# Strassen's form for the output product of an attention kernel: seven products for two batches

## The chip, the cores and the metric

The kernel runs on one core of one Trainium2 chip. Its time is the device time of one execution in microseconds (us). The engines are named as the profile names them: PE (TensorE, matrix products), PEld (its weight loads), DVE (VectorE), ACT (ScalarE), POOL (GpSimd) and SP (SyncE, whose queue issues nearly all DMAs). All data is fp32.

## What is computed

64 batches of 128 tokens with 512 features pass through a multi-query attention with one null key, and are added to their input. There are 16 heads of 64, with keys and values shared by all heads.

```python
xn = layernorm(x, g_in)                       # x: 64 x 128 x 512
q = (xn @ Wq).reshape(b, n, 16, 64).transpose(0, 2, 1, 3) * 64 ** -0.5
k, v = split(xn @ Wkv)                        # one key head, one value head
k = concat([null_kv[0], k]); v = concat([null_kv[1], v])
sim = einsum('bhid,bjd->bhij', q, k) + concat([null_bias, attn_bias])
sim = where(causal or masked, -max, sim)
out = einsum('bhij,bjd->bhid', softmax(sim), v)
y = out.transpose(0, 2, 1, 3).reshape(b, n, 1024) @ Wo     # 1024 x 512
return x + layernorm(y, g_out)
```

The change concerns the second last line, the output product, and the layer norm after it.

## The kernel before

The order of all instructions is written out by hand: `step(n)` issues one step of a software pipeline, and each engine runs its own instructions strictly in the order in which `step` names them. One step holds work of several batches: the end of batch n-1 (output product, norm, residual, store), the values of batch n, the softmax of batch n+1, the scores of batch n+2, and the keys, values, token norms and loads of later batches. Query products are made for groups of four batches (GB = 4); `part` is the step's place in its group, and `qg` the group whose queries are being made.

The query product is already in Strassen's form with seven products (`product(g, f, k, ...)`, k from 1 to 7): operands are sums of weights (`wS`) and of tokens (`xS`, made by `token_sum` on POOL), the results are put together through PSUM accumulation, copies by ACT (`keep`, names p1, u2, u3) and additions by DVE (`q_out`). Below, q1 to q7 are these.

The names that matter around the change:

- `scores(b, hf)`: one half of the score rows on PE into a PSUM tile of pool `ps_s`, then DVE adds it to the bias (L495) and takes the row maxima (L496). `KEYS` says which half: 128 keys (`UK`, L474) or 64 keys (`LK`, L485). Before, half 0 is the one of 128 keys. `ps_s` has two buffers of two banks each.
- `bias_add(b)` (POOL, L445) writes bias plus mask into the score tile `S[b]`, and `null_copy(b)` (POOL, L454) the null key's columns, ahead of the scores.
- `exps(b, hf)` (ACT, L505): eight rows, each an exponential with a sum. `rinv` (DVE, L522) inverts the sums, `scale` (POOL, L526) multiplies the half by them.
- `blocks_T(b)` (DVE, L541) transposes `S[b]` in blocks of 32 into `sb`, and `blocks_move(b)` issues 14 DMAs on SP (L561) that put the blocks into `aTb`, of which there is one.
- `values(b)`: PE products of `aTb` (L610), ACT copies them to `oT[b]` (L618).
- `out_mm(b)` (PE, L630): eight 128 x 128 by 128 x 512 products of `oT[b]` and `wo` into one PSUM bank `py`. Each fp32 product appears in the trace as two instructions.
- `out_stats(b)`: DVE statistics of `py` (L637 to L641), the reciprocal root on POOL (L642), and one fused DVE pass that subtracts the mean and multiplies by the gain `gob` (L644). `residual(b)`: ACT multiplies by the reciprocal root (L658), POOL adds the input tile `res` (L659). `store(b)` issues the DMA.
- `norm_stats`, `norm_apply` (ACT, L249): the norm of the input tokens. `tokens_T`, `tokens_out`, `tokens_in`: their transposition through DRAM. `mask_neg` (DVE, L438): the mask of a group.

PSUM has eight banks: four for `ps_s`, two for `ps_q` (tags a and c), two for `ps_w` (tag w: the query product 2, `py`, the values and the key/value block in turn).

Of the kernel before, what the change touches and what calls it, by code (L numbers as in the profile page):

```python
# [8 lines left out]
FP = mybir.dt.float32  # L9
# [8 lines left out]
def kernel(  # L18
# [49 lines left out]

    nc = tc.nc
    B, N, DIM = x.shape
    H = attn_bias.shape[0]
    DH = w_kv.shape[1] // 2
    P = 128
# [19 lines left out]

    ctx.enter_context(tc.manual_schedule())
    const = ctx.enter_context(tc.tile_pool(name="const", bufs=1))
    ps_s = ctx.enter_context(tc.tile_pool(name="ps_s", bufs=2, space=PSUM))
    ps_q = ctx.enter_context(tc.tile_pool(name="ps_q", bufs=1, space=PSUM))
    ps_w = ctx.enter_context(tc.tile_pool(name="ps_w", bufs=2, space=PSUM))  # L100
    xp = ctx.enter_context(tc.tile_pool(name="xp", bufs=XB))
    rp = ctx.enter_context(tc.tile_pool(name="rp", bufs=2))
# [17 lines left out]
    gp = ctx.enter_context(tc.tile_pool(name="gp", bufs=2))  # L120

    def loads_late(n):
        if 0 <= n:
            load_res(n)
        for m in (n + 13, n + 14):
            if m < B and (m > 2 * GB + 2) == (m == n + 14):
                load_x(m)
# [212 lines left out]
    HK, HT, HF = KC // 2, TOK // 2, H * DH // 2  # L340
    lo_k, hi_k = slice(0, HK), slice(HK, KC)
    lo_t, hi_t = slice(0, HT), slice(HT, TOK)
    wS = const.tile([P, 4, HK, HF], FP, name="wS")
    a11, a12 = wq[:, lo_k, 0:HF], wq[:, hi_k, 0:HF]
    a21, a22 = wq[:, lo_k, HF:], wq[:, hi_k, HF:]
    s1, s2, s3, s4 = (wS[:, i] for i in range(4))
    xS, prod, kept = {}, {}, {}

    def q_tile(g):
# [20 lines left out]
        )  # L370

    def weight_sums():
        nc.vector.tensor_tensor(s3, a11, a21, ALU.subtract)
        nc.vector.tensor_tensor(s1, a21, a22, ALU.add)
        nc.vector.tensor_tensor(s2, s1, a11, ALU.subtract)
        nc.vector.tensor_tensor(s4, a12, s2, ALU.subtract)

    def token_sum(g, k):

# [41 lines left out]
    def q_out(g, c, toks, tag, name=None):  # L421
        lo = toks.start // N
        o = q_part(g, c, lo, lo + 2)
        p = prod[tag].rearrange("p (t h i) -> p t h i", t=2, h=2)
        if name is None:
            nc.scalar.copy(o, p)  # L426
        else:
            k = kept[name].rearrange("p (t h i) -> p t h i", t=2, h=2)
            nc.vector.tensor_tensor(o, p, k, ALU.add)  # L429


# [25 lines left out]
        )  # L457


    KEYS = UK, LK  # L460
    WITH_NULL = slice(1 + NL, ROW), slice(0, 1 + NL)

    def scores(b, hf):
        g, t = divmod(b, GB)
        nk = N if hf == 0 else NL
        ps = ps_s.tile([P, 2, NF, N], FP, tag="s", name=f"ps_{b}_{hf}")
        pv = ps.rearrange("p r f j -> p r (f j)")[:, :, 0 : NF * nk].rearrange(
            "p r (f j) -> p r f j", f=NF
        )
        for f in range(NF):  # L470
            if hf == 0:
                for r in range(2):
                    rows = slice(r * DH, (r + 1) * DH)
                    nc.tensor.matmul(  # L474
                        pv[:, r, f, :],
                        qT[g][rows, f, t, 1].rearrange("p u i -> p (u i)"),
                        kT[b][rows, :],
                        start=True,
                        stop=True,
                    )  # L480
            else:
                for r in range(2):
                    rows = slice(r * DH, (r + 1) * DH)
                    for u in range(2):
                        nc.tensor.matmul(  # L485
                            pv[u * DH : (u + 1) * DH, r, f, :],
                            qT[g][rows, f, t, 0, u],
                            kT[b][rows, 0:NL],
                            start=True,
                            stop=True,  # L490
                        )
        if hf == 0:
            nmax[b] = small.tile([P, 2, R8], FP, tag="nmax", name=f"nmax_{b}")
        sv = S[b][:, :, KEYS[hf]].rearrange("p (r f) j -> p r f j", r=2)
        nc.vector.tensor_tensor(sv, pv, sv, ALU.add)  # L495
        nc.vector.tensor_reduce(  # L496
            nmax[b][:, hf], S[b][:, :, WITH_NULL[hf]], AX.X, ALU.max, negate=True
        )

    def exps(b, hf):  # L500
        if hf == 0:
            rsum[b] = small.tile([P, 2, R8], FP, tag="rsum", name=f"rsum_{b}")
        for k in range(R8):
            row = S[b][:, k, WITH_NULL[hf]]
            nc.scalar.activation(  # L505
                row,
                row,
                AF.Exp,
                bias=nmax[b][:, hf, k : k + 1],
                accum_out=rsum[b][:, hf, k : k + 1],  # L510
            )
# [115 lines left out]
    def out_mm(b):  # L627
# [4 lines left out]
            )  # L632
        ys[b] = py

    def out_stats(b):
        st = small.tile([P, 6], FP, tag="st", name=f"sto_{b}")
        nc.vector.bn_stats(st, ys[b])  # L637
# [2 lines left out]
        rstd = small.tile([P, 1], FP, tag="rstdo", name=f"rstdo_{b}")  # L640
        nc.vector.tensor_scalar(rstd, mv[:, 1:2], EPS, None, ALU.add)  # L641
        nc.gpsimd.tensor_tensor(rstd, rstd, nhalf, ALU.pow)  # L642
        y = hp.tile([P, DIM], FP, tag="y", name=f"y_{b}")
        nc.vector.scalar_tensor_tensor(  # L644
            y, ys.pop(b), mv[:, 0:1], gob, ALU.subtract, ALU.mult
        )
# [56 lines left out]
    def step(n):  # L703
# [6 lines left out]
        q, f = ok(qg, NG), part  # L710
        last_g, last_f = divmod(n + 5, GB)
        fast, last = q and qg > 0, 0 < last_g < NG


        fill = n <= 0
        if part == 0 and ok(qg + 1, NG) and n + 6 >= 0:
            load_mask(qg + 1)
        if ok(n + 2) and n >= 0:
            bias_add(n + 2)
        for m in mns:  # L720
            norm_stats(m)
        if fast and f == 0:
            token_sum(qg, 1)
            if fill:
                for k in range(2, 5):
                    token_sum(qg, k)
        if n == -4:
            bias_add(0)
            bias_add(1)
        if ok(n + 2):  # L730
            null_copy(n + 2)
        if 2 * GB <= mb < B:
            tokens_T(mb)
            if (mb + 1) % GB == 0:
                tokens_out(mb // GB)
        if (n + 7) % GB == 0 and 2 <= (n + 7) // GB < NG:
            tokens_in((n + 7) // GB)
        if ok(n + 1) and not fill:
            exps_half(n + 1, 0)
            exps_half(n + 1, 1)  # L740
        if ok(n - 1):
            out_mm(n - 1)
            out_stats(n - 1)
        if fast and f == 0 and not fill:
            for k in range(2, 5):
                token_sum(qg, k)
        if last:
            product(last_g, last_f, 4, ps_q, "a", start=False)
            q_out(last_g, HC + last_f, lo_t, "a")
            product(last_g, last_f, 3, ps_q, "c", start=False)  # L750
            q_out(last_g, last_f, hi_t, "c", "u2")
        if ok(n + 1) and fill:
            exps_half(n + 1, 0)
        for m in mns:
            norm_apply(m)
        if part == 3 and ok(n + 3):
            nulls_move((n + 3) // GB, slice(0, GB - 1))
        if part == 0 and ok(n + 2):
            nulls_move((n + 2) // GB, slice(GB - 1, GB))
        if fast:  # L760
            if f == 0:
                q_tile(qg)
            product(qg, f, 2, ps_w, "w")
            product(qg, f, 1, ps_q, "a")
            keep("a", "p1")
            q_out(qg, f, lo_t, "w", "p1")
            product(qg, f, 5, ps_q, "c")
        elif q:
            q_plain(qg, 2 * f)
        if ok(n + 1) and fill:  # L770
            exps(n + 1, 1)
        if ok(n - 1) and q:
            residual(n - 1)
        if ok(n + 2):
            scores(n + 2, 0)
            if not q and n + 1 < B - 2:
                blocks_T(n + 1)
            if ok(n + 1) and fill:
                rinv(n + 1, 1)
                scale(n + 1, 1)  # L780
            scores(n + 2, 1)
        if n == B - 2:
            attn_T_pe(n)
        if ok(n):
            values(n)
        if ok(n - 1) and not q:
            residual(n - 1)
        if n + 1 in sbs:
            blocks_move(n + 1)
        if fast:  # L790
            product(qg, f, 6, ps_q, "a", start=False)
            keep("a", "u2")
        elif q:
            q_plain(qg, 2 * f + 1)
        if n + 10 < 2 * GB:
            norm_T(n + 10)
        if ok(mkv) and mkv >= GB - 1:
# [1 line left out]
            pk = ps_w.tile([P, KVN + N], FP, tag="w", name=f"pk_{mkv}")  # L799
            k_T(mk, pk[:, KVN:])  # L800
            kv_mm(mkv, pk[:, 0:KVN])
        if ok(n - 1):
            store(n - 1)
        loads_late(n)
        if ok(n + 1) and q and not fill:
            blocks_T(n + 1)
            blocks_move(n + 1)
        if ok(mkv) and mkv >= GB - 1:
            kT_out(mk, pk[:, KVN:])
            kv_out(mkv, pk[:, 0:KVN])  # L810
        if fast:
            product(qg, f, 7, ps_q, "a", start=False)
            keep("a", "u3")
        if ok(mk) and not ok(mkv):
            kT_out(mk, k_T(mk))
        if fast:
            q_out(qg, HC + f, hi_t, "c", "u3")
        if ok(n + 1) and fill:
            blocks_T(n + 1)
            blocks_move(n + 1)  # L820
        if n == -4:
            for m in range(GB - 1):
                kv_out(m, kv_mm(m))
                if m:
                    kT_out(m - 1, k_T(m - 1))
        if part == 3 and 0 < qg < NG:
            mask_neg(qg)

    def keep_busy(k):
# [95 lines left out]
```

## Time and profile before

| | us |
|---|---|
| median of three runs | 1198.63 |
| the three runs | 1196.96 to 1199.11 |
| the profiled execution | 1194.94 |
| its span in the profile | 1193.1 |
| PE busy in the span | 1151.9 (97%) |
| DVE, ACT, POOL busy | 716.2, 652.1, 654.4 |

The mean granted clock of PE was 0.991 of full speed. In a line of the page's groups or of the groups by form stand the source line, the engine, the operation, the tiles written and read, the shapes and the count; then total busy time and the mean in ns of one instruction; then the engine's idle time just before them with what ended it. A line of the timeline has start, length (both in us), engine, line, operation, tiles, shape and count of merged instructions. A line of the table by windows has the window, its length, the busy time of PE, PEld, DVE, ACT and POOL with counts, the clock, the DMA share and GB/s.

### The profile page before, as it was taken

The numbers are of one execution on the slowest core, as the hardware profiler recorded it, in microseconds if no ns is written. First come the engines' busy times: TensorE is split into PE (matmuls) and PEld (weight loads), VectorE is DVE, ScalarE is ACT, GpSimd is POOL, SyncE is SP. The second block draws the span as 40 slices with busy tenths as digits, with TensorE's granted clock in tenths as the row PEclk, the third lists the DMA queues.
The fourth block names the chain that finished last, engine by engine and source line by source line (L and its number), as shares of the span: only waits on it lengthen the run. The fifth ranks groups of instructions, "written<-read, shape, count | busy, mean of one in ns | idle before, by whom it ended". The sixth has DMA issues, their size and how long they took to land.

```text
span 1193.1 us, 22640 instructions
## 1 busy us (share of the span) xinstructions
PE 1151.9 (97%) x7588; PEld 747.9 (63%) x7588; DVE 716.2 (60%) x1449; ACT 652.1 (55%) x2625; POOL 654.4 (55%) x524
## 2 busy tenths in 40 slices
PE   6888999999999999999999999999999999999887
PEld 4465666666666666666666666666666666666433
DVE  6565566566666656656665665666566565545552
ACT  2254555565565556556555655655665565555551
POOL 5453755556475555647555465746546574654641
PEclk9998999999999999999999999999999999999999
DMA  6314334343533434343343434334353433422221
GB/s 185 111 39 127 96 124 122 119 122 90 143 95 122 121 112 130 90 136 103 122 115 116 131 91 133 105 123 111 111 140 90 130 99 106 102 74 71 70 81 45
DMA packets 107844, 129.79 MB, mean 109 GB/s; under 512 B 29264, under 2 KB 72528, under 8 KB 105936
## 3 DMA queue, kind: packets, MB, share of 16 engines
q1 hardware_dynamic: 106912, 127.29, 37.2%
q8 instruction: 61, 1.00, 0.4%
q10 hardware_dynamic: 816, 1.05, 0.2%
q14 instruction: 55, 0.45, 0.1%
HBM read 54.86 MB, written 31.46 MB: 72 GB/s over the span
## 4 chain that ended last, share of the span: by engine, by line
PE 86%; SPq 4%; DVE 2%; DMA 1%; issue 1%; ACT 0%; POOL 0%; DVEq 0%; ACTq 0%
PE py L630 35%; PE pa L408 17%; PE pc L408 8%; PE po L610 8%; PE ps L474 5%; PE pk L298 5%; PE pw L408 4%; SPq L561 4%; PE ps L485 3%; DMA aTb<-sb 1%; DVE sb L541 1%; PE pk L332 1%; DMA res<-in_x_dram 0%; DVE s L495 0%; PE paL L582 0%
## 5 line engine op out<-in xcount | busy, mean ns | idle before, releaser
L630 PE MATMUL py<-wo,oT 128*128 128x512 f32 x1024 | 453.6, 596 | 1.9 <-ACT oT L618 1.9
L445 POOL TENSOR_TENSOR s<-biasp,mneg 128x1536 f32<-128x1536 f32 x64 | 220.8, 3451 | 292.6 <-DVE sb L541 193.6
L505 ACT ACTIVATE s<-s,nmax 128x129 f32<-128x129 f32 (+1 forms) x1024 | 368.8, 365 | 0.0
L630 PEld LDWEIGHTS py<-wo,oT 128*128 128x128 f32 x1024 | 195.3, 191 | 223.9 <-issue 217.0
L526 POOL TENSOR_TENSOR s<-s,rinv 128x1024 f32<-128x1024 f32 (+1 forms) x128 | 188.4, 1479 | 15.5 <-DVE rinv L522 11.3
L505 ACT ACTIVATION_READ_ACCUMULATOR s<-s,nmax 128x1 f32 x1024 | 194.1, 190 | 0.0
L618 ACT ACTIVATE oT<-po,nv 128x512 f32<-128x512 f32 x128 | 81.3, 685 | 185.3 <-PE po L610 185.1
L495 DVE TENSOR_TENSOR s<-ps,s 128x1024 f32<-128x1024 f32 (+1 forms) x128 | 121.7, 951 | 68.9 <-PE ps L474 66.0
L659 POOL TENSOR_TENSOR y<-y,res 128x512 f32<-128x512 f32 x63 | 80.3, 1274 | 151.0 <-ACT y L658 151.0
L522 DVE RECIPROCAL rinv<-rsum 128x8 f32<-128x8 f32 x128 | 25.9, 203 | 209.7 <-ACT s L505 208.2
L408 PE MATMUL pa<-xS,wS 128*128 128x256 f32 x480 | 130.6, 395 | 0.7 <-ACT ku L419 0.7
L496 DVE TENSOR_REDUCE nmax<-s 128x8 f32<-128x1032 f32 (+1 forms) x128 | 123.1, 962 | 4.4
L610 PE MATMUL po<-aTb,vs 128*64 128x256 f32 (+1 forms) x768 | 109.8, 393 | 1.8 <-DVE aTb L589 1.7
L541 DVE STREAM_TRANSPOSE sb<-s 128x1536 f32<-128x1536 f32 x62 | 109.7, 1769 | 0.1
L419 ACT COPY ku<-pa 128x256 f32<-128x256 f32 x120 | 44.7, 373 | 116.1 <-PE pa L408 114.5
L408 PEld LDWEIGHTS pa<-xS,wS 128*128 128x128 f32 x480 | 83.0, 191 | 30.3 <-issue 20.0
L249 ACT ACTIVATE x<-x,nmr,rstd 128x512 f32<-128x512 f32 x60 | 48.7, 813 | 86.3 <-DVE nmr L248 85.9
L429 DVE TENSOR_TENSOR qT<-pw,kp 128x256 f32<-128x256 f32 x60 | 25.5, 425 | 98.5 <-ACT kp L419 98.5
L474 PEld LDWEIGHTS ps<-kT,qT 64*128 64x128 f32 x1024 | 62.5, 188 | 22.5 <-issue 21.8
L474 PE MATMUL ps<-kT,qT 64*128 64x128 f32 x1024 | 74.9, 286 | 0.0
L426 ACT COPY qT<-pa 128x256 f32<-128x256 f32 x60 | 22.4, 372 | 92.1 <-PE pa L408 92.1
L637 DVE BATCH_NORM_STATS2 sto<-py 128x6 f32<-128x512 f32 x64 | 44.8, 699 | 44.6 <-PE py L630 44.5
(90 smaller groups left out, 1547.4 us busy)
## 6 DMA issues: line engine op xcount, KB each, us to landing
aTb<-sb SPq DMA_DIRECT2D x372, 64.0 KB
x<-in_x_dram SPq DMA_DIRECT2D x64, 256.0 KB
res<-in_x_dram SPq DMA_DIRECT2D x64, 256.0 KB
out_dram<-y SPq DMA_DIRECT2D x64, 256.0 KB
aTb<-sb SPq DMA_DIRECT2D x496, 32.0 KB
xd<-xb SPq DMA_DIRECT2D x14, 1024.0 KB
xT<-xd SPq DMA_DIRECT2D x56, 256.0 KB
wo<-in_L_cond_Wo_dram SPq DMA_DIRECT2D x1, 2048.0 KB
```

Source lines behind the costliest of these rows:

```text
L408: nc.tensor.matmul(prod[tag], w[:, kc, f * P : (f + 1) * P], t[:, :, kc, :], start=(start and kc == 0), stop=(kc == HK - 1), skip_group_ch ...
L445: nc.gpsimd.tensor_tensor(S[b][:, :, 1 : ROW - 1], biasp, mneg[g][:, t].unsqueeze(1).broadcast_to([P, R8, NL + N]), ALU.add,)
L474: nc.tensor.matmul(pv[:, r, f, :], qT[g][rows, f, t, 1].rearrange("p u i -> p (u i)"), kT[b][rows, :], start=True, stop=True,)
L495: nc.vector.tensor_tensor(sv, pv, sv, ALU.add)
L496: nc.vector.tensor_reduce(nmax[b][:, hf], S[b][:, :, WITH_NULL[hf]], AX.X, ALU.max, negate=True)
L505: nc.scalar.activation(row, row, AF.Exp, bias=nmax[b][:, hf, k : k + 1], accum_out=rsum[b][:, hf, k : k + 1],)
L526: nc.gpsimd.tensor_tensor(sv, sv, rinvs.pop((b, hf)).unsqueeze(2).broadcast_to([P, R8, sv.shape[2]]), ALU.mult,)
L541: nc.vector.transpose(sb.rearrange("p j e q -> p e j q"), S[b][:, :, 1 : ROW - 1].rearrange("p e (j k) -> p e j k", k=Q),)
L610: nc.tensor.matmul(po[u][r * DH : (r + 1) * DH, half], vals, aTb[rows, slots, r * NF : (r + 1) * NF], start=True, stop=True,)
L618: nc.scalar.activation(oT[b][:, u * NF : (u + 1) * NF, :].rearrange("p f (s q) -> p s f q", q=Q), po[u].rearrange("p h i f q -> p (h i) f q"),
L630: nc.tensor.matmul(py, oT[b][:, c, :], wo[:, c, :], start=(c == 0), stop=(c == NC - 1))
L659: nc.gpsimd.tensor_tensor(y, y, res.pop(b), ALU.add)
```

## The change

Batches 1 to 60 are taken in pairs (p, p+1) with p odd. Their output products become one product of a 256 x 1024 matrix with a 1024 x 512 one, cut into two by two blocks: the rows by batch, the 1024 features in two halves of four chunks, the 512 outputs in two halves of 256. Strassen's form (Winograd's variant) needs seven block products of four 128 x 128 by 128 x 256 pieces each, where the plain form has eight. Batches 0, 61, 62 and 63 keep the plain form (`plain`).

The work of a pair is spread over three steps: products 1 and 2 in step p+1 (`first`), then in step p+2 (`second`) the sums of the stationary operands on POOL (`out_sums`, four passes over 128 x 512, in place in `oT`) and products 5, 6, 7 and 3, and in step p+3 (`third`) product 4, the norms and the residuals of both batches. So odd steps hold four of the products, even steps three.

What else moves:

- The results are put together in tags X and Y of a new PSUM pool `ps_y` (two banks), in ACT copies (yp1, yp5, one half of an output tile), one DVE copy (yu2) and three DVE additions (`out_part`). `ps_s` shrinks to one buffer for that.
- Of a paired batch the norm is no longer one fused DVE pass from PSUM and an ACT scale: ACT applies mean and scale (`pair_norm`), and POOL multiplies by `gob` and adds `res` (`pair_residual`).
- The 64-key half of the scores comes first now (`KEYS` is turned round), with the values between the two halves, and the exponentials are interleaved with the products.
- In odd steps `bias_add` and `null_copy` come behind the out_sums and the first `scale`, and `blocks_T` comes ahead of the scores' DVE work. In odd steps the query product 2 comes first.
- Token sums 1 and 2 of a group move to the end of the step before; 3 and 4 stay in the group's first step, ahead of the residuals on POOL.
- `load_res` of a paired batch comes a step later. The weight sum s3 is made in place on POOL; four sums of output weights (`wT`) are made on POOL in steps 0 to 3.

The diff, cut to its core:

```diff
-    ps_s = ctx.enter_context(tc.tile_pool(name="ps_s", bufs=2, space=PSUM))
+    ps_s = ctx.enter_context(tc.tile_pool(name="ps_s", bufs=1, space=PSUM))
     ps_q = ctx.enter_context(tc.tile_pool(name="ps_q", bufs=1, space=PSUM))
+    ps_y = ctx.enter_context(tc.tile_pool(name="ps_y", bufs=1, space=PSUM))
...
-    KEYS = UK, LK
+    KEYS = LK, UK
...
+    def out_sums(p):
+        yS[p] = bp.tile([P, HC, N], FP, tag="yS", name=f"yS_{p}", bufs=1)
+        h11, h12 = oT[p][:, lo_c], oT[p][:, hi_c]
+        h21, h22 = oT[p + 1][:, lo_c], oT[p + 1][:, hi_c]
+        nc.gpsimd.tensor_tensor(yS[p], h21, h22, ALU.add)
+        nc.gpsimd.tensor_tensor(h21, h11, h21, ALU.subtract)
+        nc.gpsimd.tensor_tensor(h11, yS[p], h11, ALU.subtract)
+        nc.gpsimd.tensor_tensor(h12, h12, h11, ALU.subtract)
+
+    def out_product(p, k, pool, tag, start=True):
...
+            1: lambda: (a[:, lo_c], e11),
+            2: lambda: (a[:, hi_c], e21),
+            3: lambda: (a[:, hi_c], e22),
+            4: lambda: (b[:, hi_c], wT[:, 3]),
+            5: lambda: (yS[p], wT[:, 0]),
+            6: lambda: (a[:, lo_c], wT[:, 1]),
+            7: lambda: (b[:, lo_c], wT[:, 2]),
...
+    def pair_norm(b):
+        mv, rstd = yn.pop(b)
+        nmr = small.tile([P, 1], FP, tag="nmro", name=f"nmro_{b}")
+        nc.vector.tensor_scalar(nmr, mv[:, 0:1], rstd, -1.0, ALU.mult, ALU.mult)
+        nc.scalar.activation(ys[b], ys[b], AF.Identity, bias=nmr, scale=rstd)
+
+    def pair_residual(b):
+        nc.gpsimd.tensor_tensor(ys[b], ys[b], gob, ALU.mult)
+        nc.gpsimd.tensor_tensor(ys[b], ys[b], res.pop(b), ALU.add)
```

The new order in `step`, as it stands in steps with paired batches and query work (`soft` is true there):

```python
if second: out_sums(p5673)
elif ok(n + 2) and n >= 0: bias_add(n + 2); null_copy(n + 2)
...
if third: out_product(p4, 4, ps_y, "X", start=False)
...
if fast and n % 2: product(qg, f, 2, ps_w, "w")
if last: product(last_g, last_f, 4, ps_q, "a", start=False)
exps(n + 1, 0, 0, 4)
if third: out_part(p4 + 1, 0, "X")
if last: q_out(... "a"); product(... 3 ...); q_out(... "c", "u2")
if third: pair_stats(p4 + 1)
...
exps(n + 1, 0, 4); rinv(n + 1, 0); scale(n + 1, 0)
if second: bias_add(n + 2); null_copy(n + 2)
if first: out_product(p12, 1, ps_y, "X")
if fast and n % 2 == 0: product(qg, f, 2, ps_w, "w")
exps(n + 1, 1, 0, 2)
if second: out_product(p5673, 5, ps_y, "Y"); out_keep("Y", "yp5", "u3")
exps(n + 1, 1, 2, 4)
if first: out_keep("X", "yp1", "p1"); out_product(p12, 2, ps_w, "w"); out_part(p12, 0, "w", "yp1")
if not second: exps(n + 1, 1, 4); rinv(n + 1, 1); scale(n + 1, 1)
if fast: product(qg, f, 1, ps_q, "a"); keep("a", "p1"); q_out(qg, f, lo_t, "w", "p1")
if second: out_product(p5673, 6, ps_y, "X", start=False); out_keep("X", "yu2", "yu2")
if second: exps(n + 1, 1, 4); rinv(n + 1, 1); scale(n + 1, 1)
for m in mns: norm_apply(m)
if third: pair_norm(p4); pair_norm(p4 + 1)
if fast and f == 0: token_sum(qg, 3); token_sum(qg, 4)
if third: pair_residual(p4); pair_residual(p4 + 1)
if fast: product(qg, f, 5, ps_q, "c")
if f == GB - 1: token_sum(qg + 1, 1)
if second:
    out_product(p5673, 7, ps_y, "X", start=False); out_part(p5673 + 1, 1, "X", "yp5")
    out_product(p5673, 3, ps_y, "Y", start=False)
    if part == 3: mask_neg(qg)
    blocks_T(n + 1)
    out_part(p5673, 1, "Y", "yu2")
scores(n + 2, 0)
if second: pair_stats(p5673)
else: blocks_T(n + 1)
values(n)
blocks_move(n + 1)
scores(n + 2, 1)
product(... 6 ...); keep("a", "u2")
...
store(p4); store(p4 + 1); loads_late(n)          # stores in third
product(... 7 ...); keep("a", "u3"); q_out(qg, HC + f, hi_t, "c", "u3")
```

## The prediction

> **What bounds the kernel now.** I read the page first: engine shares, the chain that ended last, the costliest groups.
>
> ```profile
> PE 1151.9 (97%) x7588; PEld 747.9 (63%) x7588; DVE 716.2 (60%) x1449; ACT 652.1 (55%) x2625; POOL 654.4 (55%) x524
> ...
> PE 86%; SPq 4%; DVE 2%; DMA 1%; issue 1%; ACT 0%; POOL 0%; DVEq 0%; ACTq 0%
> ...
> L630 PE MATMUL py<-wo,oT 128*128 128x512 f32 x1024 | 453.6, 596 | 1.9 <-ACT oT L618 1.9
> ...
> L541 DVE STREAM_TRANSPOSE sb<-s 128x1536 f32<-128x1536 f32 x62 | 109.7, 1769 | 0.1
> ```
>
> TensorE is 86% of the chain and every other engine has 40% spare. The two durations are modelled ends, so I took pitches (start to start) from the timeline of TensorE in the middle of the run.
>
> ```profile
> 608.26 7.03 PE L630 MATMUL py<-wo,oT 128*128 128x512 f32 x16
> 615.12 1.03 PE L408 MATMUL pa<-xS,wq 128*128 128x256 f32 x4
> 615.99 1.03 PE L408 MATMUL pc<-xT,wS 128*128 128x256 f32 x4
> ...
> 618.58 1.03 PE L408 MATMUL pc<-xS,wS 128*128 128x256 f32 x4
> ```
>
> An output product takes 615.12 - 608.26 = 6.87 us; a query product of four instructions 0.865, so 0.216 for 256 columns. The next py starts at 625.71: a step is 17.45 us, without a gap.
>
> Then GpSimd, which the change loads: its groups by form and a stretch of its timeline.
>
> ```profile
> L445 POOL TENSOR_TENSOR s<-biasp,mneg 128x1536 f32<-128x1536 f32 x64 | 220.8, 3451 | 292.6 <-DVE sb L541 193.6 <-DVE mneg L438 99.1
> ...
> L526 POOL TENSOR_TENSOR s<-s,rinv 128x1024 f32<-128x1024 f32 x64 | 122.0, 1906 | 4.8 <-DVE nmr L248 2.7 <-DVE rinv L522 2.1
> ...
> L659 POOL TENSOR_TENSOR y<-y,res 128x512 f32<-128x512 f32 x63 | 80.3, 1274 | 151.0 <-ACT y L658 151.0
> ...
> 59.93 1.27 POOL L390 TENSOR_TENSOR xS<-xT 128x512 f32<-128x512 f32 x1
> 61.27 1.27 POOL L390 TENSOR_TENSOR xS<-xT,xS 128x512 f32<-128x512 f32 x1
> 62.50 1.27 POOL L390 TENSOR_TENSOR xS<-xT 128x512 f32<-128x512 f32 x1
> ```
>
> A pass over 512 elements takes 1.27 us. The second sum reads the first: pitch 1.34. The third does not read the second: 1.23.
>
> **The change, part by part.**
>
> *Products.* Two py cost 13.73 us a pair; 7 products x 8 instructions x 0.216 cost 12.10. Gain 1.63. Of the 30 pairs, 28 have their sums in steps that still carry query work: 45.6 us. The last two fall where transfers already set the step (values wait for aTb), and count nothing.
>
> *Scalar and vector work.* A pair adds three ACT copies (0.37 each, row of L419) and four DVE passes on 256 columns (0.42, row of L429; the PSUM copy kyu lies between that and the 0.26 of the 128-column kT copy), and drops two fused DVE passes (0.74). ACT's 652.1/1193.1 x 17.45 = 9.5 us a step grow by some 0.65, DVE's 10.5 by 0.3, of a 16.6 us step: taken as hidden, except in the chain below. If that cover goes, the cost is the 1.1 us of ACT a pair.
>
> *GpSimd.* A pair gains six passes of 512: four sums and two products with gob (two residual adds were there). Busy per step was 654.4/1193.1 x 17.45 = 9.6 us; it becomes about 13.4 of 16.6. The share is no trouble; the order is.
>
> I laid out a steady pair of steps from the built program's order on each engine, zero where the even step's product 4 starts. TensorE without waits: products 4, q4, q3, 1, q2, 2 to 7.78; q1 to 8.65; q5, 64-key scores, values, 128-key scores, q6, key/value block and q7 to 15.78. Odd step: q2, q4, q3; product 5 at 18.37; q1; product 6 at 20.97; q5; product 7; product 3 from 25.29; small scores 27.11; values 27.63; large scores ready at 29.27; end 33.29. (64-key scores are 0.52, 128-key 1.09, values 1.64.)
>
> Against it, the chain that starts at q1's end, 8.65:
> - ACT copies p1 after 0.25 (as at 618.58 to 618.83), 0.37 long; DVE's sum into qT ends 0.46 later, 9.73; the three small scalars stand behind it. ACT's norm_apply starts 9.89, the first pair_norm 0.72 later; it ends 11.42.
> - GpSimd, 0.08 later: multiply 1.34, add 1.23, twice: 11.50 to 16.64.
> - out_sums, each reading or overwriting what the last one touched: 3 x 1.34 + 1.23, to 21.89. Product 5 needs the first (17.9, in time), product 6 the third (20.6, in time).
> - Behind them in the same queue: reciprocal root 0.52, first scale 1.0, bias_add 3.51, null copy 0.15, second scale 1.91 (rows of L526, L445): ends 28.98. Exps ended near 23.4, so GpSimd alone decides.
> - DVE's blocks_T waits for that scale: 29.06, 1.69 to the next issue. Queued behind it: the sum of product 3 (0.34) and the scores' add (0.68): done 31.77.
> - The scores' pool now has one buffer, so the large scores wait for that add: 31.83 against 29.27. TensorE stands 2.56 us.
>
> In every second pair the even step starts a group: two token sums (1.23 each) stand before the residuals, which start at 12.98 instead of 11.50. Product 5 then waits 1.09, and the large scores 2.95. Four steps lose 2.56 + 1.09 + 2.95 = 6.60 and gain 3.26. Over 14 such periods: +92.4 - 45.6 = +46.8.
>
> Unknowns in it: the gob multiply (none in the trace: nearest L659, 1.27; at the unit scale's 1.05 the pair gains 0.4), and the gap after a dependent pass (0 to 0.07; at 0 another 0.6). Both at their best leave about 1.5 of the 2.56; 0.3 more per boundary makes it 3.
>
> *Clock.* These waits meet the granted clock. Windows of 3.41 us on the clock's own grid, in the start and the tail of this run:
>
> ```profile
> 59.37:62.78 3.41, 1.53 (x12) 1.15 (x14) 1.15 (x3) 1.47 (x4) 3.29 (x4) 1.00 0.32 94
> 62.78:66.19 3.41, 3.41 (x49) 2.89 (x46) 1.01 (x1) 0.00 (x0) 2.37 (x3) 0.50 0.15 53
> ...
> 1120.91:1124.33 3.42, 1.90 (x13) 0.94 (x14) 3.39 (x4) 0.98 (x2) 0.00 (x0) 1.00 0.56 173
> 1124.33:1127.74 3.41, 3.41 (x5) 1.33 (x5) 1.15 (x2) 3.41 (x16) 2.43 (x2) 0.50 0.17 43
> ...
> 1144.81:1148.22 3.41, 2.14 (x52) 1.56 (x52) 3.27 (x6) 0.00 (x0) 2.40 (x3) 1.00 0.26 67
> ```
>
> The first figure after the length is TensorE's busy time, the third from the end the clock. A window with 1.90 us busy or less was followed by one at 0.50 in 6 of 8 cases in the stretches I looked at; with 2.14 or more in none. The Trainium skill ("TensorE: Matmul & The Clock Gate", What's actually happening) has the slow clock follow an idle window of about 3.4 us, so a 2.6 us wait costs nothing further: sum 1247. The rows say 1.5 us idle is enough; I take the rows. A wait of 2.6 to 3.0 puts at least 1.4 us into one grid window for all but a few per cent of phases; the slow window then costs 1.7 us, less what falls in the wait itself, about 1.5. At 6 in 8: 28 x 1.5 x 0.75 = +31.5.
>
> *Transfers and SP.* Volume is unchanged. SP issues the 14 aTb moves in 9.1 us and the last lands some 1.9 later; odd blocks_T done at 30.8 gives 41.8, needed at 46: covered, as are the two stores behind the moves, the loads behind those, and tokens_in with its token sums. Were the stores late, the next y tile would wait. No charge.
>
> *Ends.* Weight sums on GpSimd (2.4 us each, interpolated from 1.27 and 3.45) lie in idle time of the first steps or delay one product by 1 to 2 us. In the tail, out_sums stand ahead of the last score blocks: +3, between -5 and +10. Together +5.
>
> Sum on the profiled execution: 1194.9 + 46.8 + 31.5 + 5 = 1278. That execution lies 0.3% below the median of the runs shown, inside their usual scatter; I add nothing.
>
> **The rivals.**
>
> *A, 0.60: wait and slow clock, 1278* (own range 1255 to 1300). For it: both halves have rows.
>
> *B, 0.20: the wait without the slow clock, 1247.* For: the skill's rule, and two of eight windows. Against: six.
>
> *C, 0.12: faster, 1155.* GpSimd gets the odd step's second scale out before TensorE needs the score buffer. Place: the large scores' wait for DVE. It decides at 26.4 instead of 28.98: GpSimd's 17.5 us from the first residual to that scale must come down to 14.9 (13.5 in group-start pairs). Then 1194.9 - 45.6 + 5 = 1155. For: 6.5 us of that is bias and scale, which move little, but eight passes are the new shape; at 0.95 us each it would do. Against: the 512-element passes between 1.26 and 1.30 us in all rows.
>
> *D, 0.08: half the wait, no slow clock, about 1201:* every GpSimd boundary at its best. Then waits eat the gain.
>
> **Numbers.** A measurement of this kernel tells about 0.2% from no change. Faster: C and a fifth of D, 0.14; same 0.02; slower 0.84. Likeliest 1278. The range takes A but its top, B and the upper part of D: 1212 to 1305.
>
> **What would show it.** Right: the 128-key score matmuls waiting on DVE's 64-key add, some 2.5 us in odd steps; DVE's transpose waiting on GpSimd's scale; GpSimd busy without a break from the residuals to that scale; granted clock below 0.97 with 0.50 stretches; an output product at 1.73 us. Wrong: TensorE without gaps at 16.65 us a step (C), gaps at clock 1.00 (B), or values waiting for aTb (then SP's queue was mis-costed).

## The result, and the profile after

| | before | after |
|---|---|---|
| median, us | 1197.8 (4 runs) | 1287.84 (4 runs) |
| lowest to highest | 1194.33 to 1199.11 | 1283.47 to 1298.11 |
| profiled execution, its span | 1194.94, 1193.1 | 1283.47, 1281.7 |
| mean granted clock of TensorE | 0.991 | 0.956 |

The change makes the kernel 7.7% slower: ratio 1.0769, 95% interval 1.0695 to 1.0843. Medians here and below are of all executions of a kernel, while ratios, each to executions of the kernel before taken beside it, leave out those in a slower state (one of E10's six took 1896.18 us). The page of after, in the places shown of before (engine shares, the granted clock in 40 slices, the chain by engine, the groups):

```profile
PE 1144.2 (89%) x8308; PEld 910.3 (71%) x8308; DVE 730.2 (57%) x1568; ACT 681.7 (53%) x2715; POOL 897.8 (70%) x709
...
PEclk9988999999999899999999899999999999999888
...
POOL 42%; PE 27%; issue 9%; ACT 9%; DVE 6%; DMA 4%; SPq 3%; POOLq 0%; ACTq 0%; DVEq 0%
...
L487 PE MATMUL ps<-kT,qT 64*128 64x128 f32 x1024 | 89.6, 324 | 71.8 <-DVE s L508 71.8
L554 DVE STREAM_TRANSPOSE sb<-s 128x1536 f32<-128x1536 f32 x62 | 110.0, 1774 | 68.4 <-POOL s L539 68.2
...
L693 PE MATMUL pyY<-wT,yS 128*128 128x256 f32 x240 | 63.1, 409 | 24.1 <-POOL yS L673 24.1
L737 POOL TENSOR_TENSOR y<-y,gob 128x512 f32<-128x512 f32 x60 | 76.6, 1277 | 10.5 <-ACT y L734 10.5
```

TensorE was 86% of the chain and is 27%; GpSimd was 0% and is 42%. The group column behind the second bar says why: the 128-key scores (L487) stand 71.8 us for VectorE's add (L508), and VectorE's transpose (L554) stands 68.4 us for GpSimd's scale (L539). The totals are nearly alike because it is one wait passed on. Product 5 (L693 into pyY) stands 24.1 us for the first of the sums on GpSimd.

One pair of steps from the timelines, first TensorE, then GpSimd, then VectorE. The even step's product 4 starts at 615.00, which is the zero of the prediction's layout.

```profile
615.00 1.89 PE L693 MATMUL pyX<-wT,oT 128*128 128x256 f32 x8
...
638.61 1.89 PE L693 MATMUL pyX<-wT,oT 128*128 128x256 f32 x8
640.34 1.89 PE L693 MATMUL pyY<-wo,oT 128*128 128x256 f32 x8
643.23 1.08 PE L623 MATMUL po<-aTb,vs 128*64 128x256 f32 x8
647.04 1.98 PE L487 MATMUL ps<-kT,qT 64*128 64x128 f32 x16 [2.72 <-DVE s L508]
```

```profile
626.42 1.28 POOL L737 TENSOR_TENSOR y<-y,gob 128x512 f32<-128x512 f32 x1 [0.87 <-ACT y L734]
...
631.58 1.27 POOL L673 TENSOR_TENSOR yS<-oT 128x512 f32<-128x512 f32 x1
...
638.39 3.45 POOL L458 TENSOR_TENSOR s<-biasp,mneg 128x1536 f32<-128x1536 f32 x1
641.90 0.33 POOL L467 COPY s<-nv 128x16 f32<-128x16 f32 x1
642.18 2.09 POOL L539 TENSOR_TENSOR s<-s,rinv 128x1024 f32<-128x1024 f32 x1
653.75 1.28 POOL L403 TENSOR_TENSOR xS<-xT 128x512 f32<-128x512 f32 x1 [9.48 <-DMA xT<-xd]
```

```profile
644.30 1.78 DVE L554 STREAM_TRANSPOSE sb<-s 128x1536 f32<-128x1536 f32 x1 [1.79 <-POOL s L539]
646.00 0.39 DVE L716 TENSOR_TENSOR y<-pyY,kyu 128x256 f32<-128x256 f32 x1
646.31 0.67 DVE L508 TENSOR_TENSOR s<-ps,s 128x512 f32<-128x512 f32 x1
```

A bracket in a line is the engine's idle time ahead of it. GpSimd runs from 626.42 to 644.27 with no bracket after that of the first line, so it waits for nothing in that stretch. The transpose starts 0.03 us after the scale ends, and the add that frees the score buffer ends at 646.98. TensorE was ready at 644.32 and starts at 647.04. The scores then take 1.98 us where they take 1.16 at full clock, and the table by windows shows that clock (third figure from the end):

```profile
640.37:643.78 3.41, 3.41 (x55) 2.40 (x55) 1.06 (x3) 0.00 (x0) 3.35 (x3) 1.00 0.79 189
643.78:647.20 3.42, 0.70 (x8) 0.24 (x6) 2.86 (x4) 1.26 (x2) 0.49 (x1) 1.00 1.03 168
647.20:650.61 3.41, 3.41 (x20) 2.92 (x21) 2.96 (x6) 0.00 (x0) 0.00 (x0) 0.50 0.70 111
```

Where the 88.6 us of span (1281.7 - 1193.1) went can be read from the times at which the values (L610 before, L623 after) start in each step, taken from TensorE's timeline:

| stretch | before | after | difference |
|---|---|---|---|
| start, to the values at 131.04 / 133.04 | 131.0 | 133.0 | +2.0 |
| the next 52 steps, to 1040.20 / 1113.69 | 909.2 | 980.7 | +71.5 |
| end, from there to the last instruction | 152.9 | 168.0 | +15.1 |

In the 52 steps TensorE's waits, added up from its timeline, are 26 of the large (128-key) scores (67.0 us) and 13 of product 5 (13.1 us). The smaller products give back 26 x 1.63 = 42.4. That leaves 71.5 - 80.1 + 42.4 = 33.8 us. There are 19 windows of 3.41 us at 0.50 (slow windows from here on) in this stretch and none before. What one costs shows in two pairs of steps, from values to values, with the same 272 instructions on TensorE; the first has no slow window, the second has one:

```profile
209.02:246.31 37.29, 33.71 (x272) 27.46 (x265) 21.86 (x48) 20.85 (x84) 27.73 (x23) 1.00 0.36 106
436.27:475.17 38.90, 35.27 (x272) 28.75 (x264) 21.96 (x48) 20.86 (x84) 27.76 (x23) 0.96 0.32 101
```

TensorE's busy time (after the length) is 1.56 us more, so the 19 slow windows cost some 30 us. The last 4 us, 0.1 for each wait, are taken as idle time that the brackets do not count, since the ends of products are modelled.

### The profile page after: what moved, and what is told of

It is laid out like the page before. It is cut to its first block, busy times and chain, and to the rows that moved or that the text cites. A ratio compares the mean times of both kernels' runs of the same rounds, so it can differ in the third digit from the quotient of the medians.

```text
span 1281.7 us, 24562 instructions
## 1 busy us (share of the span) xinstructions
PE 1144.2 (89%) x8308; PEld 910.3 (71%) x8308; DVE 730.2 (57%) x1568; ACT 681.7 (53%) x2715; POOL 897.8 (70%) x709
## 4 chain that ended last, share of the span: by engine, by line
POOL 42%; PE 27%; issue 9%; ACT 9%; DVE 6%; DMA 4%; SPq 3%; POOLq 0%; ACTq 0%; DVEq 0%
POOL s L539 9%; PE pa L421 8%; POOL s L458 8%; ACT s L518 7%; POOL y L737 5%; PE pyX L693 5%; POOL y L738 4%; PE ps L487 4%; POOL xS L403 3%; PE pk L307 3%; POOL oT L675 3%; POOL yS L673 3%; POOL oT L674 3%; POOL oT L676 3%; PE py L643 2%
## 5 line engine op out<-in xcount | busy, mean ns | idle before, releaser
L518 ACT ACTIVATE s<-s,nmax 128x65 f32<-128x65 f32 (+1 forms) x1024 | 371.9, 368 | 2.1 <-DVE nmax L509 1.6
L539 POOL TENSOR_TENSOR s<-s,rinv 128x512 f32<-128x512 f32 (+1 forms) x128 | 191.2, 1495 | 53.8 <-DVE rinv L535 50.7
L693 PE MATMUL pyX<-wT,oT 128*128 128x256 f32 x720 | 173.6, 384 | 1.1 <-DVE rinv L535 0.6
L693 PEld LDWEIGHTS pyX<-wT,oT 128*128 128x128 f32 x720 | 137.4, 193 | 23.9 <-POOL oT L675 2.9
L487 PE MATMUL ps<-kT,qT 64*128 64x128 f32 x1024 | 89.6, 324 | 71.8 <-DVE s L508 71.8
L554 DVE STREAM_TRANSPOSE sb<-s 128x1536 f32<-128x1536 f32 x62 | 110.0, 1774 | 68.4 <-POOL s L539 68.2
L487 PEld LDWEIGHTS ps<-kT,qT 64*128 64x128 f32 x1024 | 75.6, 223 | 99.5 <-DVE s L508 85.8
L508 DVE TENSOR_TENSOR s<-ps,s 128x512 f32<-128x512 f32 (+1 forms) x128 | 120.7, 943 | 28.7 <-PE ps L487 15.9
L509 DVE TENSOR_REDUCE nmax<-s 128x8 f32<-128x520 f32 (+1 forms) x128 | 123.1, 961 | 7.8 <-POOL s L467 3.3
L421 PE MATMUL pa<-xS,wq 128*128 128x256 f32 x480 | 123.5, 380 | 1.7 <-ACT ku L432 1.7
L623 PE MATMUL po<-aTb,vs 128*64 128x256 f32 (+1 forms) x768 | 109.3, 396 | 3.5 <-DMA aTb<-sb 1.9
L421 PEld LDWEIGHTS pa<-xS,wq 128*128 128x128 f32 x480 | 87.0, 190 | 12.1 <-ACT ku L432 2.8
L693 PE MATMUL pyY<-wT,yS 128*128 128x256 f32 x240 | 63.1, 409 | 24.1 <-POOL yS L673 24.1
L737 POOL TENSOR_TENSOR y<-y,gob 128x512 f32<-128x512 f32 x60 | 76.6, 1277 | 10.5 <-ACT y L734 10.5
```

Source lines behind the costliest of these rows:

```text
L421: nc.tensor.matmul(prod[tag], w[:, kc, f * P : (f + 1) * P], t[:, :, kc, :], start=(start and kc == 0), stop=(kc == HK - 1), skip_group_ch ...
L487: nc.tensor.matmul(pv[:, r, f, :], qT[g][rows, f, t, 1].rearrange("p u i -> p (u i)"), kT[b][rows, :], start=True, stop=True,)
L509: nc.vector.tensor_reduce(nmax[b][:, hf], S[b][:, :, WITH_NULL[hf]], AX.X, ALU.max, negate=True)
L518: nc.scalar.activation(row, row, AF.Exp, bias=nmax[b][:, hf, k : k + 1], accum_out=rsum[b][:, hf, k : k + 1],)
L539: nc.gpsimd.tensor_tensor(sv, sv, rinvs.pop((b, hf)).unsqueeze(2).broadcast_to([P, R8, sv.shape[2]]), ALU.mult,)
L554: nc.vector.transpose(sb.rearrange("p j e q -> p e j q"), S[b][:, :, 1 : ROW - 1].rearrange("p e (j k) -> p e j k", k=Q),)
```

## The experiments

The theory: GpSimd's chain from the first residual to the odd step's second scale is too long, VectorE's transpose hands its lateness to the score buffer, and the slow clock follows from the wait. The rivals: the single buffer or the turned halves are at fault by themselves; the clock comes from something else; the wait just moves to the next place. A pair starts a group when its even step is the first of a group of four batches, which every second pair does; the others are called plain pairs. Lines of code are those of after where nothing else is said.

**E1: the transpose behind the scores' add.** In odd steps `blocks_T` no longer stands ahead of the add on VectorE.

```diff
         mask_neg(qg)
-            if n + 1 < B - 2:
-                blocks_T(n + 1)
             out_part(p5673, 1, "Y", "yu2")
...
+        if soft and n + 1 < B - 2:
+            blocks_T(n + 1)
         if second:
             pair_stats(p5673)
-        elif soft and n + 1 < B - 2:
-            blocks_T(n + 1)
```

> Only DVE's order changes: in odd steps blocks_T(n+1) stands behind the add and the maximum of the 64-key scores instead of ahead of them. Theory (the large scores wait because the one score buffer is read by an add that stands behind a transpose, which waits for GpSimd's second scale): that add then needs only bias_add, done about 2 us earlier, so the waits of 2.74 us before the 128-key scores vanish in all 28 odd steps (-77 us) and with them nearly all slow-clock windows (some 19 of them at 1.5 us, -28); the 0.9 us before product 5 after a group start stays. Expected about 1180, between 1165 and 1200; the aTb moves start 2 us later and may take some of it back as waits of the values. Rival 'GpSimd's load as such is the bound' (its work is unchanged here): above 1260. Rival 'the 256-column products are slower on TensorE': 1280.

Measured: 1244.36 us, ratio 1.0403 (1.037 to 1.0437). The large scores no longer wait at all, with the single buffer, the turned halves and all of GpSimd's work still there, so the hand-over by VectorE is shown. But the time is some 64 us over what was expected. Three lines of the table of waits (engine and what it waited for; us, times, longest) and one of TensorE's timeline tell where it went:

```profile
PE pyY L693 <- POOL yS L673: 42.1, 16, 3.9
...
POOL xS L403 <- DMA aTb<-sb: 62.8, 9, 9.3
...
POOL xS L403 <- DMA xT<-xd: 39.2, 5, 10.4
```

```profile
648.20 3.57 PE L693 MATMUL pyY<-wT,yS 128*128 128x256 f32 x8 [3.20 <-POOL yS L673]
```

Product 5 in pairs that start a group now mostly waits 3.1 to 3.2 us instead of 0.9. GpSimd's queue has the token sums of the next group ahead of the pair's passes, and they wait up to 10.4 us for `tokens_in` (the transfer that they wait for stands as xT or as aTb in this view; in the timeline the wait ends with xT). With TensorE 2.7 us earlier per pair, that lateness came out at the next place.

**E6: the token sums in their own step, on top of E1.** Sums 1 and 2 leave the end of the step before and come behind the first `scale` of the group's first step.

```diff
+        if fast and f == 0 and not fill:
+            token_sum(qg, 1)
+            token_sum(qg, 2)
         if second and ok(n + 2):
             bias_add(n + 2)
...
-        if f == GB - 1 and n > 0 and ok(qg + 1, NG):
-            token_sum(qg + 1, 1)
...
-        if f == GB - 1 and n > 0 and ok(qg + 1, NG):
-            token_sum(qg + 1, 2)
```

> As e1 (transpose behind the 64-key scores in odd steps), and token sums 1 and 2 go back into the first step of their own group, behind the first scale there, so that GpSimd no longer stands at the head of its queue until tokens_in has landed (it stood there 62.8 us in 9 places in e1). Theory: the wait for product 5 after a group start, 3.2 us in e1, falls to about 1, as laid out for that case in the prediction (1.09): 1244 - 14 x 2.1 - 8 slow windows at 1.5 = about 1203, between 1190 and 1220. Rival 'these waits come from GpSimd's total work, not from the transfer ahead of it': 1230 to 1245.

Measured: 1195.1 us, ratio 0.9997 (0.9983 to 1.0012). Product 5's waits fall from 42.1 to 17.4 us, the slow windows between 150 and 1100 us from 12 to 2. So E1's miss was the token sums' place. Two orders of instructions, with no operation taken away, are worth 92.7 us (1287.84 - 1195.1); the seven products then just pay for the rest.

**E2: the second scale ahead of the bias.** In odd steps `bias_add` and `null_copy` come behind the second `scale`, with the transpose left where the change put it.

```diff
-        if second and ok(n + 2):
-            bias_add(n + 2)
-            null_copy(n + 2)
...
             scale(n + 1, 1)
+        if second and ok(n + 2):
+            bias_add(n + 2)
+            null_copy(n + 2)
```

> Only GpSimd's order changes: in odd steps the second scale stands ahead of bias_add and null_copy; the work is the same. Theory: the scale ends near 25.3 of the two-step layout instead of 28.98, the transpose is done by 27.1, and the 64-key add now waits for bias_add, near 29.0: the wait before the 128-key scores falls from 2.74 to about 0.7, and windows with 1.5 us idle become rare. Expected 1283 - 28 x 2.0 - 25 = about 1202, between 1185 and 1220. Rival 'GpSimd's load as such is the bound': no change, 1275 to 1290.

Measured: 1261.95 us, ratio 1.0577 (1.0542 to 1.0612). Two odd steps of TensorE's timeline, and VectorE around the second:

```profile
227.71 1.16 PE L487 MATMUL ps<-kT,qT 64*128 64x128 f32 x16 [0.50 <-DVE s L508]
...
264.23 1.16 PE L487 MATMUL ps<-kT,qT 64*128 64x128 f32 x16 [3.22 <-DVE s L508]
```

```profile
260.96 0.64 DVE L451 TENSOR_SCALAR mneg<-m 128x256 f32<-128x256 uint8 x2 [3.28 <-POOL s L458]
261.51 1.76 DVE L554 STREAM_TRANSPOSE sb<-s 128x1536 f32<-128x1536 f32 x1
```

In the first the wait falls to 0.50 (this odd step has no `mask_neg`). In the other kind of odd step `mask_neg` stands ahead of the transpose on VectorE, and must not overwrite `mneg` before the bias pass has read it. With the pass moved back, the mask is late and everything behind it. The large scores' waits in the 52 steps fall only from 67.0 to 48.0 us, and the time stays 60 us above the 1202 expected. The edit shows the chain, and that the bias pass cannot simply be put later.

**E3: the wait filled.** Ahead of the large scores in odd steps TensorE gets six products with a matrix of zeros (added into a tile, so that they change no value).

```diff
+        if second and fast:
+            for _ in range(6):
+                nc.tensor.matmul(prod["a"], zero, wq[:, 0, 0:HT], start=False, ...)
         if ok(n + 2):
             scores(n + 2, 1)
```

> The wait stays, but TensorE is busy in it: six products of a zero matrix with wq (0.43 us each, 2.6 us) are added onto the query product in tag a between the values and the 128-key scores of odd steps with query work; they add zero. Theory of the clock (1.5 us idle in one window of 3.41 us brings a slow window): the slow windows vanish between 150 and 1100 us, the granted clock there rises from 0.97 to 1.00, and the time falls by some 17 windows at 1.5 us, to about 1257 (1250 to 1265), although TensorE has 72 us more work. Rule of a whole idle window, or a clock that has another cause: 1280 to 1295, slow windows as before.

Measured: median 1284.07, ratio 1.0728 (1.0665 to 1.079); the profiled execution took 1270.91, against 1283.47 of after. TensorE's timeline (here L967 is the filling, L489 the scores):

```profile
633.30 2.86 PE L967 MATMUL pa<-wq,zero 128*128 128x256 f32 x12
636.12 1.16 PE L489 MATMUL ps<-kT,qT 64*128 64x128 f32 x16
```

Between 150 and 1100 us the slow windows fall from 19 to 2: idle time of TensorE is the cause of the slow clock. The time is not what was expected, and the 52 steps show why. They take 969.2 us (980.7 in after). The filling takes 26 x 2.82 = 73.3 us where the waits were 67.0, so +6.3; product 5 waits 23.1 us instead of 13.1, +10.0, since GpSimd does not come earlier when TensorE runs faster; and 17 windows less at 1.56 are -26.5. That makes 970.5. So the clock's own cost is confirmed, but over a third of it went back into the other wait. The medians differ by less than their spread, and E3's lies where the rival expected it (1280 to 1295); it is the count of slow windows that speaks against the rival.

**E7: the gain on VectorE.** GpSimd's multiplication by `gob` (L737) is removed; VectorE does it in one pass with the subtraction of the mean, as before the change, and ACT only scales.

```diff
+        nc.vector.scalar_tensor_tensor(
+            ys[b], ys[b], mv[:, 0:1], gob, ALU.subtract, ALU.mult)
...
-        nc.scalar.activation(ys[b], ys[b], AF.Identity, bias=nmr, scale=rstd)
+        nc.scalar.activation(ys[b], ys[b], AF.Copy, scale=rstd)
...
-        nc.gpsimd.tensor_tensor(ys[b], ys[b], gob, ALU.mult)
```

> The change with two GpSimd passes fewer a pair: DVE subtracts the mean and multiplies by gob in one pass right behind the statistics, ACT scales, GpSimd only adds res. All orders stay. Theory: the chain from pair_norm to the second scale is 2.6 us shorter, so plain pairs wait no more (0.1 us) before the 128-key scores; pairs after a group start keep a wait of up to 2.7. 1287 - 14 x 2.7 - half of the rest - most slow windows: about 1215, between 1195 and 1235. If the chain through ACT's pair_norm or DVE decided instead of GpSimd's passes: 1275 or more.

Measured: 1251.87, ratio 1.0426 (1.0375 to 1.0477). Two neighbouring odd steps:

```profile
632.48 1.16 PE L487 MATMUL ps<-kT,qT 64*128 64x128 f32 x16 [0.24 <-DVE s L508]
...
669.88 1.88 PE L487 MATMUL ps<-kT,qT 64*128 64x128 f32 x16 [2.73 <-DVE s L508]
```

With 2.6 us taken from GpSimd's 17.5 the plain pair's wait (the first line) is 0.24 us. This is the point that the prediction gave for rival C (17.5 down to 14.9). Pairs that start a group keep 2.73, 15 of the 19 slow windows stay where most were expected to go, and the values wait 8.4 us for `aTb` in the 52 steps; the median is 36.9 us over the expected 1215.

**E5: the kernel before with one score buffer and turned halves.** No pairs, no extra GpSimd work.

```diff
-    ps_s = ctx.enter_context(tc.tile_pool(name="ps_s", bufs=2, space=PSUM))
+    ps_s = ctx.enter_context(tc.tile_pool(name="ps_s", bufs=1, space=PSUM))
...
-    KEYS = UK, LK
+    KEYS = LK, UK
...
-            scores(n + 2, 1)
...
             values(n)
+        if ok(n + 2):
+            scores(n + 2, 1)
```

> The kernel before with the score pool at one buffer, the halves turned (64 keys first) and the values between the two halves, as in the change; the output product stays plain and all else stays where it was. Theory: the add of the 64-key half (0.68 us) is over before the values (1.64 us) are, so one buffer costs nothing where DVE is free: 1190 to 1203. Rival 'the single score buffer costs by itself': 1220 or more.

Measured: 1231.59, ratio 1.0317 (1.028 to 1.0354). The rival's number came, but not by the rival's way. From the table of waits and the chain:

```profile
PE po L610 <- DMA aTb<-sb: 26.8, 24, 5.1
...
PE ps L474 <- DVE s L495: 2.5, 2, 1.7
```

```profile
PE 66%; SPq 12%; DMA 7%; DVE 4%; issue 2%; POOL 1%; ACT 1%; DVEq 0%; ACTq 0%; POOLq 0%
```

The scores hardly wait for the buffer (2.5 us in all). The values wait for `aTb` instead, 24 times (7 before): from start to start their products take 98.5 us in the 52 steps where they took 71.2, and that is all of the 27.3 us that these steps lose. SP's queue is 12% of the chain (4% before): the large half now comes last on VectorE, the transpose behind it later, and so the 14 moves. One buffer is harmless where VectorE's add is not held up. That this order of halves costs 37 us without pairs (the kernel before had 1194.93 beside it) does not carry over to after, where the transpose stands elsewhere.

**E4: the new order without pairs.** Meant to leave only the order and the single buffer of the change.

```diff
-    P_LAST = B - 5
+    P_LAST = B - 64
```

> Everything of the change but the pairs: P_LAST is 0, so every batch has the plain output product, while the single score buffer, the turned halves, the split exps and the token sums of the new order stay. Theory: none of these costs anything alone; TensorE runs without waits at 17.45 us a step: 1192 to 1202. Rival 'the single score buffer or the new order costs by itself': 1215 or more.

Measured: 1416.55, ratio 1.1848 (1.1825 to 1.1871). This is far over the expected 1192 to 1202, and a poor test of the rival. The values wait 57 times for VectorE's sum that frees tag w:

```profile
ACT qT L439 <- PE pa L421: 372.9, 60, 6.8
...
PE po L623 <- DVE qT L442: 101.8, 57, 2.4
```

With the plain output product in TensorE's queue ahead of product q4, ACT's copy of q4 waits up to 6.8 us (372.9 in all, 23.1 in after), and exponentials stand behind that copy, in an order made for pairs. E4 tells nothing of the buffer; E5 does.

**E8: E1, E6 and E7 together,** with pairs only up to batch 56 (`P_LAST = B - 9`).

> Three changes together: transpose behind the 64-key scores (e1), token sums 1 and 2 in their own group's step (e6), gain on DVE (e7), and the last four batches of the tail in the plain form (P_LAST 55 instead of 59), whose pairs waited 5.8 and 4.3 us for their first sum. Theory: no wait of TensorE is left between 150 and 1090 us, no slow window there, and the seven products bring what they save: 1195 - 45 + 5 = 1155, between 1148 and 1175. If something else holds the step (transfers, ACT), it shows as values waiting for aTb: 1180 or more.

Measured: 1187.12, ratio 0.9906 (0.9872 to 0.994): 1% faster than the kernel before, but 32 us short of the 1155. The 52 steps take 890.7 us where 26 pairs without waits would be 909.2 - 42.4 = 866.8, and the end takes 159.9.

**E9 and E10: what the end costs.** E9 is after with the plain product for the last two pairs (`P_LAST = B - 9`), E10 is E8 with those pairs put back (`B - 5`).

> The kernel after with one size changed: pairs only up to batches 55 and 56, so the last two pairs, whose sums fall into steps without query work, take the plain output product. Question: which part of the change makes the end longer. Measured from the values of batch 55's step to the last instruction, the end took 152.9 us before and 168.0 us after; in the latter product 5 of the two last pairs waits 5.82 and 4.31 us for yS. Theory (the pairs themselves, since no query product is left to fill TensorE while GpSimd makes the sums): the end falls to 156 to 160 us, the time to about 1277 (1272 to 1281). Rival (the turned halves, the single score buffer and the order around them cost the same without pairs): the end stays at 165 or more, the time within 4 us of 1284 to 1288.

> The kernel with the three edits together (transpose behind the scores' add, a group's token sums in its own step, the gain on VectorE), but with pairs up to batch 60 as in the kernel after. Question: how much of that kernel's gain on the kernel before comes from the plain end, how much from the three edits. In the three-edit kernel the end, counted as above, took 159.9 us. Theory (pairs without query work cost some 5 us each): end about 168, time about 1194, the same as before within 0.3%. Rival (the three edits also shorten the pairs of the end, as GpSimd's queue is shorter): end 160 or less, time 1187 or less.

Measured: E9 1284.11, ratio 1.0728 (1.0706 to 1.075), within 4 us of after as its rival said; but the interval of after (1.0695 to 1.0843) has room for the 10 us of the theory too, so E9 alone does not decide. E10 1173.56, ratio 0.9794 (0.9764 to 0.9823), better than its rival and 13.6 us under E8. Most of that is not the end: E10's 52 steps take 881.4 us against 890.7 in E8, with the same instructions, and why is open. The ends themselves, 158.3 us with the pairs and 159.9 without, say from one profile each that pairs do not make the end longer once GpSimd's queue is short. E10's waits on the same three places:

```profile
PE po L623 <- DMA aTb<-sb: 12.3, 4, 5.1
...
PE pyY L693 <- POOL yS L673: 2.1, 1, 2.1
...
PE ps L487 <- DVE s L508: 0.8, 1, 0.8
```

```profile
PE 74%; DVE 8%; DMA 6%; POOL 6%; SPq 3%; issue 2%; ACT 1%; DVEq 0%; POOLq 0%; ACTq 0%
```

The 71.8 us of the large scores are 0.8, GpSimd is 6% of the chain, and TensorE leads it again. E10 beats both kernels with all thirty pairs in Strassen's form. Of its 114 us against after, E1 brings 43.5, the token sums 49.3, the gain on VectorE 21.5, in that order of adding them and by medians that scatter by several us.

## Why the prediction was right, and where its sizes were off

The prediction was 1278 for the profiled execution, which took 1283.47, and it held the mechanism. By its steps:

- *Products.* Product 7 starts at 638.61 and product 3 at 640.34: 1.73 us, as predicted.
- *The GpSimd layout.* First residual pass predicted at 11.50 after the zero, measured 11.42; sums at 16.64, measured 16.58; second scale's end 28.98, measured 29.27. The 0.29 us more are that scale's 2.09 us, where the row of before had 1.91, and the null copy, 0.28 to the next start instead of 0.15. The gob multiplication, which had no row, took 1.28 against the assumed 1.27.
- *The waits.* Predicted 2.56 and 2.95 for the large scores, 1.09 for product 5. Measured about 2.74 in both kinds of pair and mostly 0.88 (1.9 and 2.0 in two of 13 pairs): 6.36 in four steps instead of 6.60.
- *The clock.* Predicted 28 x 0.75 = 21 slow windows at 1.5 us, measured 19 at 1.56. The 0.75 came from eight windows with waits of other lengths, so that it fits is in part luck. The choice against the Trainium skill ("TensorE: Matmul & The Clock Gate", What's actually happening: an idle window of about 3.4 us) was right in this trace: the window ahead of the slow one above holds 0.70 us of work, so 2.71 us idle are enough. Rival B, at 1247, lies 36 us under the measured execution. E3 shows the cause by taking the idle time away.
- *Scalar and vector work hidden.* No wait for ACT shows in the 52 steps, and VectorE is only waited for where it waits for GpSimd itself.
- *"tokens_in with its token sums: covered."* This step failed as reasoning. The sums' first pass stands 9.48 us for the transfer at the head of GpSimd's queue. In after that costs little, because TensorE waits elsewhere; E1 made it the next limit, and E6 is worth 49 us on top of E1 for removing it.
- *Ends.* Sized at +5, and the step that was mis-sized. With the stretches of the table, the prediction's rates give 72.7 us for the 52 steps (28 pairs' 78.3 x 26/28) and 10.6 for the rest, its two further pairs included. Measured 71.5 and 17.1. In the end product 5 of the last two pairs waits longest:

```profile
1192.15 3.78 PE L693 MATMUL pyY<-wT,yS 128*128 128x256 f32 x8 [5.82 <-POOL yS L673]
...
1222.28 3.78 PE L693 MATMUL pyY<-wT,yS 128*128 128x256 f32 x8 [4.31 <-POOL yS L673]
```

There are no query products left there to run while the sums are made. Taking these pairs away saves little (E9), while a shorter GpSimd queue with the pairs kept brings the end from 168.0 to 158.3 (E10); E7, where GpSimd only loses its multiplication, ends in 155.4. So most of the +15.1 is the same chain; what makes up the rest against before (152.9) was not tried.

Rival C, at 1155, is what the change would have been with GpSimd out of the way. E10 comes to 1173.56. What separates the two: the 52 steps are 14.6 us above 866.8, the end 5.4 above before and the start 2.9. By their starts, some 5 us of the steps' part are values that wait, mostly for VectorE, some 6 are single waits of query products, and 2.2 is one wait for the sums of output weights.

## What to carry to other kernels

Cheaper arithmetic on the bounding engine is worth what the helpers' order leaves of it: here 42 us of TensorE were bought with passes on a half idle GpSimd, and the price was set by what stood behind them in its queue, not by its share of busy time. Lay the helper's chain out in time against the moment the buffer is needed, follow the hand-over through the engine in between, and look at every wait at the head of that queue, since it shows only once the wait in front of it is gone. Keep an operation that waits for nothing late (the scores' add) from standing behind one that does (the transpose).

## What the runs showed of the hardware

*The clock and idle time.* I took the profiles of after, E1, E2, E3, E6, E7, E8 and E10 between 150 and 1100 us, cut them on the clock's own grid of 3.41 us, and counted for each window at full clock how long TensorE was idle in it and whether the next window had the clock at 0.50. With 2.0 us idle or more it was slow in 48 of 48 cases, with 1.5 to 2.0 in 9 of 30, with 1.0 to 1.5 in 2 of 48, with less than 1.0 in none of 2023. In E4, not among these, it was slow in 33 of 33 with 1.5 to 2.0. So the idle time within one window of the grid goes with the slow clock, with an edge between 1.5 and 2 us that these counts do not fix; a wait that the grid cuts in two can go free.

*SP's queue under load.* The 14 moves of `aTb` take 9.0 to 10.4 us on SP in 48 steps of after. In the 14 steps that have them behind the four loads of `tokens_in` they take 10.1 to 13.8 us, but for the first and the last (9.6 and 9.1). In the case below the loads were issued from 639.88 on and their data was used at 653.75, 13.9 us later. That the loads are the cause was not tried:

```profile
639.88 2.94 SPq L294 DMA_DIRECT2D xT<-xd x4
...
646.14 13.82 SPq L574 DMA_DIRECT2D aTb<-sb  x14
```
